# Two states of a selective scan in one tile, and where the last set's gating rows are kept

## The chip, the cores and the metric

The kernel runs on one core of a Trainium2 chip. A core has a matrix engine (PE, whose weight loads are listed apart as PEld), a vector engine (DVE), a scalar engine (ACT), a general engine (POOL) and a sequencer (SP) that here issues all DMAs. The engines run side by side and wait for each other by semaphores; each carries out its own instructions in the order in which they are listed. The metric is the time of one execution on the device in microseconds (us), the median of several runs.

## The reference, cut to what matters

An input of 8 batches of 512 tokens by 128 channels, x, goes through six residual blocks: an expert layer, an attention, the same expert layer, an attention with 16 gated experts (block "ea" in the kernel's names), a selective scan, and the 16 experts again ("eb"). Two of them are touched.

The scan, for each batch, with 256 channels d and 16 states n:

```
deltaA = exp(einsum('bld,dn->bldn', delta, A))
deltaB_u = (delta * u)[..., None] * Bm[:, :, None, :]
...
def step(h, t):
    dA_t, dBu_t, C_t = t
    h = dA_t * h + dBu_t
    return (h, jnp.einsum('bdn,bn->bd', h, C_t))
```

The end of the gated experts, where the attention's result is weighed by each expert's gate rw before the output product:

```
mixed = attn[:, :, None, :] * rw[..., None]
return jnp.einsum('bted,edc->btc', mixed, o_proj)
```

## The kernel before

Everything is one program for all 8 batches. The first three blocks run first (to about 360 us). After that two pipelines are interleaved: the scan of one batch after another (`scan_states`, two halves h of 128 channels each), and the expert blocks of other batches (`expert_qkv`, `expert_attend`), "ea" ahead of the scan of the same batch and "eb" behind it. The last set of all is "eb" of batch 7, named `ebg77`.

**The scan of one half** (`scan_states`, lines 936 to 1000) goes through the 16 states in 8 pairs m. For a pair, SP loads two tiles (line 967), `bn` and `cn`, each the rows of B or C of two states, repeated over 128 partitions (128x2x512, two buffers each). For each state: ACT makes `da` by an exponential (recorded at the helper's line 138), DVE multiplies the B row by `dup` into a PSUM bank `db` (line 977), DVE runs the recurrence over 512 tokens from `da` and `db` into an SBUF tile `hs` (line 980). Then POOL multiplies `hs` by its half of `cn` in place (line 983), and PE adds four transposes of it into the PSUM bank `ys` (line 986), which sums over the states. `hs` is one 128x512 tile for each state, six buffers. The generator gives up control (`yield`) after each ACT step, each DVE step, and each POOL multiplication.

**The end of an expert set** (`att_out`, lines 779 to 827): PE makes the attention output into PSUM (line 785), ACT copies it to `atT` (line 794). For each of 8 pairs m of experts, SP issues two DMAs that load the gate rows of the two experts from DRAM (`rwd`, written at line 624), each repeated over 64 partitions, into a 128x512 tile `pm` (line 803). `pm` has three buffers in the expert pool `ex`, so the loads of pair m=3 wait until the product of an earlier pair has been read. Then `mixed = pm * atT` (line 808, two buffers) on POOL; in the sets named in `QUICK`, `ebg77` among them, on DVE where m % 3 is not 0. PE multiplies `mixed` by the output weights (line 812, four token blocks for each m), DVE adds the result to x (line 822) and SP stores it (line 826).

**What sets the order.** The functions are generators, and `weave` first runs them in an order given by nominal times: each part has a start, an end and a number of steps (for `scan_states`, `3 + 4 * NS` in line 1449). `list_anew` then lists all instructions anew: it keeps a model of each engine's costs (`costs`: for POOL 2.125 ns an element and 185 ns), of buffers, and of a port that POOL and some DVE instructions share (`shares_port`), and lists each engine's instructions by the longest remaining way. One pass gives a plan, the second is built by it; so every instruction's place on its engine, and every buffer's place, comes out of this model. Buffers of the scan pool `sc` (tags `bn`, `cn`, `hs` and others) and the expert pool `ex` are tiles with fixed places, such as `bn_at0`.

Of the kernel before, what the change touches and what calls it, by code (L numbers as in the profile page):

```python
# [10 lines left out]
F32 = mybir.dt.float32  # L11
# [5 lines left out]
ALU = mybir.AluOpType  # L17
AX = mybir.AxisListType

P = 128  # L20
# [6 lines left out]

QKV_ACT = (1, 3, 5, 7)

QUICK, QKV_ACT_QUICK = ("eag00", "ebg77"), (0, 2, 4)  # L30

PART_BUFS, HS_BUFS, DA_BUFS, TAP_BUFS = 3, 3, 3, 2
# [28 lines left out]
def macaron_kernel(  # L61
# [19 lines left out]
    nc = tc.nc  # L81
    B, S, C = x_in.shape
# [5 lines left out]
    NH = 2  # L88
    NS = 16
# [37 lines left out]
    def behind(i, name, reason="table order"):  # L127
        i = getattr(i, "ins", i) if reason == "table order" else i
        order_only.append((i.name, name))
        tc.add_manual_dep(  # L130
            i,
            name,
            mybir.DependencyInfo(mybir.DependencyClass.NoSync, mybir.DependencyReason.DATA),
            reason=reason,
        )

    def act(*args, **kwargs):
        exp_ln.append(nc.scalar.activation(*args, **kwargs).ins.name)  # L138
# [321 lines left out]
    def scales_of(pool, psum, g, name, held):  # L460
        held[name, "scales"] = yield from ln_scales(pool, psum, g, name)
        yield
# [316 lines left out]
    def att_out(pool, psum, b, name, held, store):  # L779
        x, vv, den, rwd = xs[b], held[name, "vv"], held[name, "den"], held[name, "rwd"]  # L780
        sTs = [held[name, "sT", q] for q in range(J)]
        pat = psum("tr", [P, S], f"pat_{name}")
        for q in range(J):
            for k in range(q + 1):
                nc.tensor.matmul(
                    pat[:, q * P : (q + 1) * P],
                    lhsT=vv[:, k].rearrange("p i d -> p (i d)"),
                    rhs=sTs[q][:, k * P : (k + 1) * P],
                    start=k == 0,
                    stop=k == q,  # L790
                )
        yield
        atT = pool.tile([P, S], F32, tag="atT", name=f"atT_{name}", bufs=1)
        nc.scalar.copy(atT, pat)  # L794
        yield
        nc.vector.reciprocal(den, den)
        yield
        po = psum("tr", [P, J, C], f"po_{name}")
        for m in range(NE1 // 2):

            pm = pool.tile([P, S], F32, tag="pm", name=f"pm_{name}_{m}", bufs=3)
            for i in range(2):
                nc.sync.dma_start(
                    pm[i * HD1 : (i + 1) * HD1], rwd[2 * m + i : 2 * m + i + 1].to_broadcast([HD1, S])
                )
            mixed = pool.tile([P, S], F32, tag="mixed", name=f"mixed_{name}_{m}", bufs=2)
            engine = nc.vector if name in QUICK and m % 3 else nc.gpsimd
            engine.tensor_mul(mixed, pm, atT)  # L808
            yield
            for j in range(J):  # L810

                nc.tensor.matmul(  # L812
                    po[:, j, :],
                    lhsT=mixed[:, j * P : (j + 1) * P],
                    rhs=ow[:, m, :],
                    start=(m, j) == (0, 0),
                    stop=(m, j) == (NE1 // 2 - 1, J - 1),
                    skip_group_check=True,
                )
            yield  # L820
        for j in range(J):
            nc.vector.scalar_tensor_tensor(
                x[:, j, :], po[:, j, :], den[:, j : j + 1], x[:, j, :], ALU.mult, ALU.add
            )
        if store:
            nc.sync.dma_start(out[b].rearrange("(j p) c -> p j c", p=P), x)
        yield
# [108 lines left out]
    def scan_states(pool, psum, b, h, held):  # L936
        held[b, "delta", h]
        u, dl, du = (held[b, c][h] for c in ("u", "dl", "du"))
        z, bcd = held[b, "z"], held[b, "bcd"]

        ys = psum("ys", [P, J, P], f"ys_{b}_{h}")
        dup = psum("du", [P, S], f"dup_{b}_{h}")
        first = nc.scalar.copy(dup, du)
        if b + h:

            behind(first, held["late", NH * b + h - 1])
        yield

        scaled = nc.scalar.activation(u, u, AF.Copy, scale=cols[:, DSKIP + h : DSKIP + h + 1])
        behind(scaled, first.ins.name)  # L950
        for j in range(J):
            nc.tensor.matmul(
                ys[:, j, :],
                lhsT=u[:, j * P : (j + 1) * P],
                rhs=ident,
                is_transpose=True,
                start=j == 0,
                stop=False,
                skip_group_check=True,
            )  # L960
        yield
        for m in range(NS // 2):
            bn, cn = (
                pool.tile([P, 2, S], F32, tag=f"{c}n", name=f"{c}n_{b}_{h}_{m}", bufs=2) for c in "bc"
            )
            for t, r in ((bn, 2 * m), (cn, NS + 2 * m)):
                nc.sync.dma_start(
                    t, bcd[r : r + 2, :].rearrange("n s -> (n s)").unsqueeze(0).to_broadcast([P, 2 * S])
                )
            hs = [pool.tile([P, S], F32, tag="hs", name=f"hs_{b}_{h}_{m}_{i}", bufs=2 * HS_BUFS) for i in range(2)]  # L970
            for i in range(2):
                n = 2 * m + i
                db = psum("mm", [P, S], f"db_{b}_{n}_{h}")
                da = pool.tile([P, S], F32, tag="da", name=f"da_{b}_{n}_{h}", bufs=DA_BUFS)
                act(da, dl, AF.Exp, scale=a_neg[:, h * NS + n : h * NS + n + 1])
                yield
                product = nc.vector.tensor_mul(db, bn[:, i, :], dup)  # L977
                if n == NS - 3:
                    held["late", NH * b + h] = product.ins.name
                nc.vector.tensor_tensor_scan(hs[i], da, db, 0.0, ALU.mult, ALU.add)  # L980
                yield
            for i in range(2):
                nc.gpsimd.tensor_mul(hs[i], hs[i], cn[:, i, :])  # L983
                yield
                for j in range(J):
                    nc.tensor.matmul(  # L986
                        ys[:, j, :],
                        lhsT=hs[i][:, j * P : (j + 1) * P],
                        rhs=ident,
                        is_transpose=True,  # L990
                        start=False,
                        stop=(m, i, j) == (NS // 2 - 1, 1, J - 1),
                        skip_group_check=True,
                    )
            if m == NS // 2 - 1:
                yield
                zh = z[:, :, h * P : (h + 1) * P]
                nc.vector.tensor_mul(zh, ys, zh)
                held[b, "yz", h] = True
            yield  # L1000
# [438 lines left out]
    def scan_parts(pool, psum, t, b, held):  # L1439
        pieces = [(0.05, 0.0, 1, scan_normed(pool, psum, b, held)), (0.1, 0.0, 1, scan_begin(pool, b, held))]  # L1440
        for h in range(NH):
            pieces.append((0.15 + 0.1 * h, 0.0, 1, scan_conv(pool, psum, b, h, held)))
        for i in range(2):
            pieces.append((0.35 + 0.1 * i, 0.45 + 0.1 * i, 3, scan_gate(psum, b, i, held)))
        pieces += [(0.55, 0.0, 1, scan_rows(pool, psum, b, held)), (0.6, 0.0, 1, scan_rank(pool, psum, b, held))]
        pieces.append((0.7, 0.0, 1, scan_silu(b, held)))
        for h in range(NH):
            pieces.append((0.8 + 0.1 * h, 0.0, 1, scan_delta(pool, psum, b, h, held)))
        states = [(0.5 * h, 0.5 + 0.5 * h, 3 + 4 * NS, scan_states(pool, psum, b, h, held)) for h in range(NH)]
        states += [(1.0 + 0.02 * h, 0.0, 1, scan_turn(pool, psum, b, h, held)) for h in range(NH)]  # L1450
        states += [(1.04, 1.12, J + 2, scan_finish(psum, b, held))]
        return (
            [(t - 0.24 * SLOT_T, t - 0.24 * SLOT_T, 1, scales_of(pool, psum, (b,), f"ss{b}", held))]
            + spread(t - 0.22 * SLOT_T, t, pieces)
            + spread(t, t + SLOT_T, states)
        )
# [12 lines left out]
    def psum(tag, shape, name):  # L1469
        return psp.tile(shape, F32, tag="bank", name=name, bufs=8)  # L1470
# [12 lines left out]
    sc = Buffers(behind_pools(first, "sc", "left"), dict(xn=1, xps=1))  # L1483
# [110 lines left out]
    parts, held, t = [], Held(), 0.0  # L1594
# [79 lines left out]
```

## Time and profile before

| what | value |
|---|---|
| median of 3 runs (lowest to highest) | 1281.96 us (1279.81 to 1287.47) |
| profiled execution: its own time, its span | 1279.87 us, 1278.1 us |
| busy in the span: PE, DVE, POOL, ACT | 1101.5, 1065.3, 935.9, 851.5 us |
| POOL multiplications at line 983 | 256 of 1280 ns |
| DVE scans at line 980 | 256 of 1210 ns |
| busy in 400 to 1200 us (800 us): PE, DVE, POOL | 690.3, 714.0, 673.4 us |
| granted PE clock, mean | 0.929 |

A row of the page's groups has the line, engine and operation, what is written and read, the shape, the count, then the busy time and the mean of one, then the idle time of the engine just before such instructions and what ended most of it. A row of the timeline has start, length, engine, line, operation and count, and in square brackets the idle time before it and who ended it. The chain is the sequence of waits and work that ended last, followed back from the end.

### The profile page before, as it was taken

Reading aid. Unit: us, or ns where it says so; the run is one execution under the profiler, and the core shown is the slowest. Engines: PE = TensorE matmul, PEld = TensorE weight load, DVE = VectorE, ACT = ScalarE, POOL = GpSimd, SP = SyncE. Lnnn points to the kernel's source line nnn. Section 1 sums busy time; section 2 is a strip of 40 time slices with the busy share of each in tenths; the row PEclk is TensorE's granted clock in tenths of the full one; section 3 lists DMA queues with packets and bytes.
Section 4 is the critical chain, followed back from the end, with each engine's and each line's share of the span. In section 5 each row is a group of like instructions: output and inputs, shape, how many; then the busy total and the mean of one; then the engine's idle time right before and its main releaser. Section 6 shows DMA issues by size and latency. Waiting matters only on the chain.

```text
span 1278.1 us, 20254 instructions
## 1 busy us (share of the span) xinstructions
PE 1101.5 (86%) x6242; PEld 907.4 (71%) x6242; DVE 1065.3 (83%) x2613; ACT 851.5 (67%) x1953; POOL 935.9 (73%) x784
## 2 busy tenths in 40 slices
PE   6988899999897877788989989899897769988875
PEld 5767778678675765666868878687785657777665
DVE  7997666987789999998989979989985998899462
ACT  4788873675587778565886687686577458865321
POOL 5685532764489898883999889789989857888641
PEclk9999998999899998896999989799998969989797
DMA  5000000000175776754556646545765872476211
GB/s 150 25 9 1 1 1 1 1 28 22 47 218 197 215 248 213 235 183 134 190 177 210 216 147 215 168 149 205 232 202 169 259 238 96 132 236 209 79 65 50
DMA packets 69215, 178.05 MB, mean 139 GB/s; under 512 B 9585, under 2 KB 18162, under 8 KB 69106
## 3 DMA queue, kind: packets, MB, share of 16 engines
q1 hardware_dynamic: 69106, 176.75, 43.0%
q8 instruction: 49, 0.80, 0.3%
q14 instruction: 60, 0.49, 0.1%
HBM read 173.57 MB, written 3.15 MB: 138 GB/s over the span
## 4 chain that ended last, share of the span: by engine, by line
PE 30%; DVE 27%; ACT 16%; POOL 10%; issue 9%; DMA 6%; SPq 1%; POOLq 0%; DVEq 0%; ACTq 0%
PE bank_at L251 15%; DVE hs_at L980 9%; DVE bank_at L977 5%; DVE qkv_at L661 3%; POOL hs_at L983 3%; PE bank_at L986 3%; PE bank_at L812 2%; ACT part_at L675 2%; DVE x L436 2%; DMA bn_at<-bcd 2%; POOL sums_at L690 2%; ACT my_at L440 2%; PE bank_at L358 2%; DMA pm_at<-rwd_ebg 2%; ACT da_at L138 1%
## 5 line engine op out<-in xcount | busy, mean ns | idle before, releaser
L983 POOL TENSOR_TENSOR hs_at<-hs_at,cn_at 128x512 f32<-128x512 f32 x256 | 323.8, 1280 | 73.7 <-DVE hs_at L980 23.0
L980 DVE TENSOR_TENSOR_SCAN hs_at<-da_at,bank_at 128x512 f32<-128x512 f32 x256 | 306.2, 1210 | 5.1 <-PE bank_at L986 1.2
L138 ACT ACTIVATE da_at<-dl_at,a_neg 128x512 f32<-128x512 f32 x256 | 184.8, 725 | 104.7 <-DVE hs_at L980 100.4
L675 ACT ACTIVATE part_at<-bank_at,rw_at 128x192 f32<-128x192 f32 x496 | 177.8, 424 | 83.4 <-PE bank_at L251 70.1
L986 PE MATMUL bank_at<-ident,hs_at 128*128 128x128 f32 x1024 | 181.7, 298 | 33.9 <-POOL hs_at L983 32.4
L808 POOL TENSOR_TENSOR mixed_at<-pm_at,atT_at 128x512 f32<-128x512 f32 x118 | 150.9, 1287 | 54.6 <-ACT atT_at L794 27.0
L661 DVE SCALAR_TENSOR_TENSOR qkv_at<-bank_at,rw_at,qkv_at 128x192 f32<-128x192 f32 x464 | 174.2, 408 | 19.0 <-PE bank_at L251 12.9
L977 DVE TENSOR_TENSOR bank_at<-bn_at,bank_at 128x512 f32<-128x512 f32 x256 | 172.3, 686 | 20.5 <-DMA bn_at<-bcd 6.0
L690 POOL TENSOR_TENSOR sums_at<-sums_at,part_at 128x768 f32<-128x768 f32 x92 | 170.1, 1848 | 20.5 <-ACT part_at L675 19.0
L812 PE MATMUL bank_at<-ow,mixed_at 128*128 128x128 f32 x1024 | 163.6, 298 | 21.7 <-POOL mixed_at L808 20.6
L986 PEld LDWEIGHTS bank_at<-ident,hs_at 128*128 128x128 f32 x1024 | 133.0, 153 | 55.8 <-POOL hs_at L983 50.3
L812 PEld LDWEIGHTS bank_at<-ow,mixed_at 128*128 128x128 f32 x1024 | 146.8, 207 | 33.4 <-POOL mixed_at L808 30.6
L251 PE MATMUL bank_at<-pw_hi,xha_at 128*128 128x384 f32 x256 | 98.5, 402 | 20.2 <-DVE hs_at L980 8.6
L251 PE MATMUL bank_at<-pw_hi,xhb_at 128*128 128x384 f32 x256 | 97.1, 400 | 11.5 <-DVE rw_at L609 2.9
L446 POOL TENSOR_TENSOR my_at<-my_at,my_at 128x512 f32<-128x512 f32 x48 | 62.4, 1302 | 39.4 <-ACT my_at L440 35.2
L440 ACT ACTIVATE my_at<-bank_at,moe_w_at 128x128 f32<-128x128 f32 x256 | 71.9, 401 | 27.1 <-PE bank_at L251 23.8
L251 PE MATMUL bank_at<-pw_lo,xha_at 128*128 128x384 f32 x256 | 85.0, 348 | 0.0
L251 PE MATMUL bank_at<-pw_hi,xla_at 128*128 128x384 f32 x256 | 83.9, 352 | 0.0
L251 PE MATMUL bank_at<-pw_lo,xhb_at 128*128 128x384 f32 x256 | 83.9, 344 | 0.0
L436 DVE SCALAR_TENSOR_TENSOR x<-bank_at,moe_w_at,x 128x128 f32<-128x128 f32 x256 | 78.0, 342 | 6.9 <-PE bank_at L251 6.0
L251 PE MATMUL bank_at<-pw_hi,xlb_at 128*128 128x384 f32 x256 | 79.7, 344 | 0.0
L863 POOL TENSOR_TENSOR u_at<-u_at,tap_at 128x511 f32<-128x511 f32 (+1 forms) x48 | 61.4, 1279 | 24.9 <-issue 16.0
(269 smaller groups left out, 2614.4 us busy)
## 6 DMA issues: line engine op xcount, KB each, us to landing
bn_at<-bcd SPq DMA_DIRECT2D x128, 512.0 KB, 4.5
cn_at<-bcd SPq DMA_DIRECT2D x128, 512.0 KB, 4.6
pm_at<-rwd_eag SPq DMA_DIRECT2D x128, 128.0 KB, 3.6
pm_at<-rwd_ebg SPq DMA_DIRECT2D x128, 128.0 KB, 3.4
x<-x_in_dram SPq DMA_DIRECT2D x8, 256.0 KB, 4.4
out_dram<-x SPq DMA_DIRECT2D x8, 256.0 KB, 2.9
pw<-proj_w_dram SPq DMA_DIRECT2D x6, 256.0 KB, 2.8
ew<-expert_w_dram SPq DMA_DIRECT2D x1, 512.0 KB, 6.4
```

The lines of the kernel that those rows point to most:

```text
L138: exp_ln.append(nc.scalar.activation(*args, **kwargs).ins.name)
L251: nc.tensor.matmul(out, lhsT=lhs[a], rhs=rhs[b], start=first and k == 0, stop=final and k == 2)
L436: nc.vector.scalar_tensor_tensor(x[:, j, :], pe[:, i, :], w[:, j, k : k + 1], x[:, j, :], ALU.mult, ALU.add)
L661: nc.vector.scalar_tensor_tensor(qkv, v, rw[:, i : i + 1], qkv, ALU.mult, ALU.add)
L675: nc.scalar.activation(held[name, "parts", h][i][:, j, :], pp[:, i, :], AF.Copy, scale=rw[:, i : i + 1])
L690: nc.gpsimd.tensor_add(sums, sums, t)
L808: engine.tensor_mul(mixed, pm, atT)
L812: nc.tensor.matmul(po[:, j, :], lhsT=mixed[:, j * P : (j + 1) * P], rhs=ow[:, m, :], start=(m, j) == (0, 0), stop=(m, j) == (NE1 // 2 - 1, ...
L977: product = nc.vector.tensor_mul(db, bn[:, i, :], dup)
L980: nc.vector.tensor_tensor_scan(hs[i], da, db, 0.0, ALU.mult, ALU.add)
L983: nc.gpsimd.tensor_mul(hs[i], hs[i], cn[:, i, :])
L986: nc.tensor.matmul(ys[:, j, :], lhsT=hs[i][:, j * P : (j + 1) * P], rhs=ident, is_transpose=True, start=False, stop=(m, i, j) == (NS // 2 ...
```

## The change

In `scan_states` the two states of a pair get one tile `hs` of 128x2x512 (three buffers, so the same bytes); each scan writes its half; POOL multiplies the whole tile by the whole of `cn` in one instruction, after both scans; then come the transposes of both states, eight for each bank. The nominal number of steps becomes `3 + 3 * NS`. In `att_out`, for `ebg77` alone, the rows `pm` are put two pairs to a tile of the shape and tags of `bn` and `cn` in the scan pool: four tiles hold all eight pairs.

```
+LAST = "ebg77"
...
-            pm = pool.tile([P, S], F32, tag="pm", name=f"pm_{name}_{m}", bufs=3)
+            if name == LAST:
+
+                if not m % 2:
+                    c = "bc"[m // 2 % 2]
+                    pms = sc.tile([P, 2, S], F32, tag=f"{c}n", name=f"pm_{name}_{m}", bufs=2)
+                pm = pms[:, m % 2, :]
+            else:
+                pm = pool.tile([P, S], F32, tag="pm", name=f"pm_{name}_{m}", bufs=3)
...
-            hs = [pool.tile([P, S], F32, tag="hs", name=f"hs_{b}_{h}_{m}_{i}", bufs=2 * HS_BUFS) for i in range(2)]
+            hs = pool.tile([P, 2, S], F32, tag="hs", name=f"hs_{b}_{h}_{m}", bufs=HS_BUFS)
...
-                nc.vector.tensor_tensor_scan(hs[i], da, db, 0.0, ALU.mult, ALU.add)
+                nc.vector.tensor_tensor_scan(hs[:, i, :], da, db, 0.0, ALU.mult, ALU.add)
                 yield
+            nc.gpsimd.tensor_mul(hs, hs, cn)
+            yield
             for i in range(2):
-                nc.gpsimd.tensor_mul(hs[i], hs[i], cn[:, i, :])
-                yield
                 for j in range(J):
                     nc.tensor.matmul(
                         ys[:, j, :],
-                        lhsT=hs[i][:, j * P : (j + 1) * P],
+                        lhsT=hs[:, i, j * P : (j + 1) * P],
...
-        states = [(0.5 * h, 0.5 + 0.5 * h, 3 + 4 * NS, scan_states(pool, psum, b, h, held)) for h in range(NH)]
+        states = [(0.5 * h, 0.5 + 0.5 * h, 3 + 3 * NS, scan_states(pool, psum, b, h, held)) for h in range(NH)]
```

## The prediction

> **What bounds the kernel now.** I read the page from the top: busy shares, the chain that ended last, the costliest groups. Then the busy times by stretch, who waits for whom between 400 and 1200 us (the scan), and the timeline of the last 53 us.
>
> ```profile
> PE 1101.5 (86%) x6242; PEld 907.4 (71%) x6242; DVE 1065.3 (83%) x2613; ACT 851.5 (67%) x1953; POOL 935.9 (73%) x784
> PE 30%; DVE 27%; ACT 16%; POOL 10%; issue 9%; DMA 6%; SPq 1%; POOLq 0%; DVEq 0%; ACTq 0%
> L983 POOL TENSOR_TENSOR hs_at<-hs_at,cn_at 128x512 f32<-128x512 f32 x256 | 323.8, 1280 | 73.7 <-DVE hs_at L980 23.0
> L980 DVE TENSOR_TENSOR_SCAN hs_at<-da_at,bank_at 128x512 f32<-128x512 f32 x256 | 306.2, 1210 | 5.1 <-PE bank_at L986 1.2
> L690 POOL TENSOR_TENSOR sums_at<-sums_at,part_at 128x768 f32<-128x768 f32 x92 | 170.1, 1848 | 20.5 <-ACT part_at L675 19.0
> L986 PE MATMUL bank_at<-ident,hs_at 128*128 128x128 f32 x1024 | 181.7, 298 | 33.9 <-POOL hs_at L983 32.4
> ```
>
> No engine is the bound alone. PE, DVE and POOL are all near full in the scan and the chain changes between them. POOL holds 10% of it, and the page gives 3% of the span (38 us) to line 983. DVE almost never waits for an `hs` buffer (1.2 us in all).
>
> ```profile
> core 0: us, PE busy (x) PEld busy (x) DVE busy (x) ACT busy (x) POOL busy (x), PEclk, DMA share, GB/s
> 700.00:800.00 100.00, 93.58 (x592) 79.48 (x591) 87.38 (x199) 73.23 (x167) 90.44 (x68) 0.97 0.60 191
> 800.00:900.00 100.00, 91.44 (x541) 76.67 (x541) 93.00 (x194) 72.36 (x160) 83.88 (x64) 0.93 0.56 180
> 900.00:1000.00 100.00, 87.52 (x529) 72.16 (x529) 80.18 (x133) 69.42 (x145) 90.42 (x69) 0.93 0.61 195
> ```
>
> From one 100 us stretch to the next the busiest engine changes: DVE at 800 to 900, POOL at 900 to 1000.
>
> The second edit lies in the tail, where little else runs:
>
> ```profile
> 1230.67 38.26 SPq L803 DMA_DIRECT2D pm_at<-rwd_ebg  x16
> 1258.98 1.77 POOL L808 TENSOR_TENSOR mixed_at<-pm_at,atT_at 128x512 f32<-128x512 f32 x1 [18.67 <-ACT atT_at L794]
> 1262.05 0.69 DVE L808 TENSOR_TENSOR mixed_at<-pm_at,atT_at 128x512 f32<-128x512 f32 x1 [2.42 <-PE bank_at L812]
> 1265.27 1.26 POOL L808 TENSOR_TENSOR mixed_at<-pm_at,atT_at 128x512 f32<-128x512 f32 x1 [4.53 <-DMA pm_at<-rwd_ebg]
> 1270.29 1.26 POOL L808 TENSOR_TENSOR mixed_at<-pm_at,atT_at 128x512 f32<-128x512 f32 x1 [3.75 <-DMA pm_at<-rwd_ebg]
> 1271.61 2.05 PE L812 MATMUL bank_at<-ow,mixed_at 128*128 128x128 f32 x16 [0.45 <-POOL mixed_at L808]
> ```
>
> The sixteen loads are spread over 38 us because they wait for the three `pm` buffers, and POOL's products of m=3 and m=6 wait for rows (4.53 and 3.75 us). The chain runs through both waits.
>
> **First edit: one POOL instruction for two states.** What does it save? Instructions that follow each other directly overlap a little, so I use the distance between starts:
>
> ```profile
> 700.67 1.83 POOL L687 TENSOR_TENSOR sums_at<-part_at,part_at 128x768 f32<-128x768 f32 x1
> 702.47 1.27 POOL L808 TENSOR_TENSOR mixed_at<-pm_at,atT_at 128x512 f32<-128x512 f32 x1
> 703.71 4.97 POOL L983 TENSOR_TENSOR hs_at<-hs_at,cn_at 128x512 f32<-128x512 f32 x4
> ```
>
> A 128x768 takes 702.47 - 700.67 = 1.80 us, a 128x512 703.71 - 702.47 = 1.24 us, and four in 4.97 us agree, (4.97 - 1.28)/3 = 1.23. So 256 elements more cost 0.56 us, and 128x1024 should take 1.24 + 2 x 0.56 = 2.36 us against 2.48 us for two: 0.12 us saved for a pair, and 128 pairs make 15 us of POOL's 936. By the durations (1848 - 1280 = 568 ns for 256) it is 2560 - 2416 = 144 ns a pair, 18 us.
>
> Not all of this reaches the end. The least: only where line 983 is on the chain, 38 us / 2.48 = 15 pairs x 0.12 = 1.8 us. The most: POOL binds everywhere, 15 us. I take the share of the scan in which POOL is busier than DVE by these rows, the two stretches 700 to 800 and 900 to 1000 out of eight: 15 x 2/8 = 3.8 us, which is nearest to the chain's value.
>
> What does it cost? A product now waits for both scans. The first state's transposes come later by one DVE product and one scan, 0.69 + 1.21 = 1.90 us, and by the longer instruction, 2.36 - 1.24 = 1.12 us, together 3.0 us; the second state's, where POOL is free, by 1.12 us. On PE, all that is listed behind these transposes waits with them; the profile has this wait already (32.4 us in 37 waits between 400 and 1200 us). Behind the longer POOL instruction, other POOL work (the sums at line 690, `mixed`, the taps) can be held up to 1.12 us longer. SP's next load of `cn` starts when the product has been read, 1.12 us later, but the row itself is needed 1.90 us later, so POOL's 18.2 us of waits for `cn` should not grow. `hs` buffers: a pair lives from its first scan to its last transpose, two (scan + product) 3.8, POOL 2.36, eight transposes of 0.27 or 2.2: about 8.4 us; three pairs last 3 x 6.25 = 18.8 us at the mean pace of 32 states in 100 us. So DVE's wait for `hs` stays small; without that slack each late pair would cost DVE, the busiest engine of the stage, its 3.0 us directly.
>
> In the longest pieces of the chain I find a scan followed directly by its line 983 five times (412, 522, 605, 887, 907 us). Bounds of the cost: 0 if PE has other work each time; 5 x 1.12 = 5.6 us if none. I take the half, 2.8 us. Far off lies the case that PE starves; it is a rival below.
>
> The changed generator and the changed step count also make the listing place all instructions anew. The trace can't show what another order gives; I bound it by two neighbouring stretches, DVE busy 93.0 against 80.2 in 100 us: one such stretch won or lost is 13 us either way. I put it at zero, the middle, and keep half, 6.5 us, as the width of the forecast.
>
> One rule speaks against longer POOL instructions. In the tail POOL's product took 1.77 us instead of 1.28 while DVE ran one with two SBUF inputs (1258.93). The Trainium skill, "SBUF — State Buffer", section "SBUF: two separate sides", says that such a DVE instruction and a POOL one take turns at a shared port pair, held for the whole instruction. By it a 2.36 us product would block DVE for up to 2.36 us. But during the scan DVE's products, scans and line 661 each read one operand from PSUM, so by the rule the sum gets nothing.
>
> **Second edit: all rows of the last set at once.** The rows in DRAM are written by line 624 at 1227.42; the first load follows at 1230.67. The last scan's readers of `bn` and `cn` end at 1191, so the four places are free. Sixteen issues of 0.45 to 0.60 us end near 1239, and with 3.4 us to land all rows are there by 1243, long before `atT` (1258.93); an issue is hidden under 15 us of qkv matmuls, and without that cover it would cost its 8.6 us. Only the last store is behind them on SP.
>
> What is late next is the two `mixed` buffers. PE takes 1.0 us for one m (2.05 us for two). Following on from the rows of before: m=2 on DVE at 1262.05 as now; m=3 on POOL when PE has done m=1, 1263.0 to 1264.3, PE to 1265.3; m=4 on DVE at 1264.0, PE to 1266.4; m=5 at 1265.4, PE to 1267.4; m=6 on POOL when m=4 is done, 1266.45 to 1267.7, PE to 1268.8; m=7 to 1269.8. PE now ends at 1271.61 + 2.05 = 1273.66: gain 3.9 us. Bounds: 0 if the order of before stays bound elsewhere, 4.9 if PE ran eight times 1.0 us without a gap from 1260.80.
>
> **Sum** against the profiled execution's 1279.87 us (2.1 below the median 1281.96): -3.8 + 2.8 - 3.9 = -4.9, so 1275.
>
> **The rivals.** *PE starves (slower).* Place: PE's in-order queue at line 986. If half of the 37 waits, 18, grow by 3.0 us without other work, that is 55 us, and with PE's 30% of the chain 16.5 us: 1279.87 + 16.5 - 3.9 = 1292. It decides from the point where these waits outweigh the gains: (3.8 + 3.9) / (0.3 x 3.0) = 9 such waits. For it: PE and PEld wait for line 983 longer than for nearly anything else. Against: PE has idle time in the scan, 800 - 690 = 110 us, and work of other batches.
>
> *POOL binds everywhere.* All 15 us and the tail: 1279.87 - 15 - 3.9 = 1261. For it: POOL at 90% in three stretches. Against: DVE is busier over the whole scan, 714 against 673 us in 800.
>
> *The second edit does nothing.* The `mixed` buffers or a later place in the listing hold the tail as it is: 1275 + 3.9 = 1279. Against: `DMA` ends the two waits, and the loads fit by 16 us.
>
> **How the numbers follow.** Forecast 1275, own range 1268 to 1282 (6.5 either way): 0.45. PE starves, 1292, spread 1286 to 1300: 0.25. POOL binds, 1261, spread 1255 to 1268: 0.20. Tail unchanged, 1279: 0.10. About 1% is what a measurement of this kernel can tell from no change; against 1281.96 that is below 1269.1 or above 1294.8. Faster: all of the POOL rival and 0.10 of the forecast's lower edge, 0.30. Slower: 0.17 of PE starving. Same: 0.53. The range leaves out 0.08 of the POOL rival and 0.12 of PE starving: 1258 to 1296.
>
> **What would show it.** Line 983: 128 rows of 128x1024 near 2.4 us (2.5 or more refutes the saving). POOL busy near 918 to 921. PE's waits for line 983 in 400 to 1200 us: near 32 us in the forecast, over 60 if PE starves. SP's sixteen loads at line 803 in under 10 us, no wait of POOL for `pm` in the tail, and PE's products at line 812 from first to last in 9.0 us instead of 12.9. DVE's wait at line 980 for line 986 over 10 us would mean that three pair buffers are too few. The prediction is wrong if the scan's stretch (360 to 1190 us) moves by more than 10 us: then the order of the listing, not the instruction's price, decides.

## The result, and the profile after

| | before | changed |
|---|---|---|
| median | 1281.26 us (1279.81 to 1287.47, 4 runs) | 1310.56 us (1308.25 to 1315.68, 4 runs) |
| ratio to before, 95% interval | | 1.0232 (1.0203 to 1.0261) |
| profiled execution: time, span | 1279.87, 1278.1 us | 1309.9, 1308.1 us |

The change is 29 us slower; the forecast was 1275 and its range ended at 1296. In the changed kernel the scan is at line 988, POOL's product at 990, the transposes at 994, `mixed` at 816, its matmuls at 820, the loads of `pm` at 811. From its page, busy times, chain by engine, and groups:

```profile
PE 1103.1 (84%) x6242; PEld 913.5 (70%) x6242; DVE 1071.4 (82%) x2613; ACT 852.7 (65%) x1953; POOL 917.4 (70%) x656
PE 31%; DVE 28%; ACT 18%; issue 10%; POOL 7%; DMA 5%; SPq 1%; POOLq 0%; DVEq 0%; ACTq 0%
L990 POOL TENSOR_TENSOR hs_at<-hs_at,cn_at 128x1024 f32<-128x1024 f32 x128 | 303.7, 2374 | 94.6 <-DVE hs_at L988 54.1
L988 DVE TENSOR_TENSOR_SCAN hs_at<-da_at,bank_at 128x512 f32<-128x512 f32 x256 | 306.0, 1210 | 2.7 <-PE bank_at L252 0.6
L994 PE MATMUL bank_at<-ident,hs_at 128*128 128x128 f32 x1024 | 176.1, 304 | 54.5 <-POOL hs_at L990 54.3
```

The work of PE, DVE and ACT is the same within 1%, and POOL's is 18.5 us less: 128 products of 2374 ns for 256 of 1280. No engine's work accounts for the 30 us of span: they are time in which the engines stand. Over the same 800 us of the scan each does less than before (of POOL's 36 us some are the merger's own saving).

```profile
core 0: us, PE busy (x) PEld busy (x) DVE busy (x) ACT busy (x) POOL busy (x), PEclk, DMA share, GB/s
400.00:1200.00 800.00, 668.29 (x3939) 557.19 (x3939) 699.28 (x1391) 549.31 (x1182) 637.31 (x373) 0.91 0.59 189
```

(Before: PE 690.3, DVE 714.0, POOL 673.4; the granted clock, 0.91, is the same in both. Over the whole span it was 0.929 and 0.920.)

The waits around the product, two rows before and two after, with the total in us, the number of waits and the longest, from 400 to 1200 us:

```profile
PE bank_at L986 <- POOL hs_at L983: 32.4, 37, 3.1
POOL hs_at L983 <- DVE hs_at L980: 22.7, 16, 3.0
```

```profile
PE bank_at L994 <- POOL hs_at L990: 48.5, 38, 3.0
POOL hs_at L990 <- DVE hs_at L988: 54.1, 18, 18.1
```

PE's waits for the products grew by 16 us. POOL's waits for the scans grew by 31 us in almost as many waits; one of them is 18.1 us long.

Where in time? The end of a half scan, the product at line 998 before and 1006 after, is a good mark. Start in us, from the timelines:

| half scan | 1st | 6th | 9th | 11th | 16th | end of span |
|---|---|---|---|---|---|---|
| before | 413.9 | 644.2 | 827.3 | 942.4 | 1192.9 | 1278.1 |
| changed | 422.0 | 672.5 | 831.5 | 965.8 | 1225.4 | 1308.1 |
| difference | 8.1 | 28.3 | 4.2 | 23.4 | 32.5 | 30.0 |

The loss is not spread evenly, as a dearer step in each pair would be: it jumps, falls back and jumps again. And it begins before the scan. The rows of line 980 before and of 988 after, with the first and last start:

```profile
L980 DVE TENSOR_TENSOR_SCAN hs_at<-da_at,bank_at x256: 1190/1210/1222, 365.3 to 1186.9; 128x512 f32<-128x512 f32 x128
```

```profile
L988 DVE TENSOR_TENSOR_SCAN hs_at<-da_at,bank_at x256: 1192/1210/1223, 372.3 to 1217.8; 128x512 f32<-128x512 f32 x128
```

The first scan starts 7.0 us later, after 365 us of a program in which the change touches no instruction. Part of this can be the difference between two executions. In the four profiles whose kernels keep the order of before (before itself and three runs of the next section) it starts at 365.3 to 367.3 us, in the four with the changed kernel's order (itself and three such runs) at 371.3 to 372.6: some 4 us or more come from the order. The longest gap between the two scans of a pair, on the timelines of DVE and POOL after, lies in one of the jumps:

```profile
834.58 1.21 DVE L988 TENSOR_TENSOR_SCAN hs_at<-da_at,bank_at 128x512 f32<-128x512 f32 x1
...
850.99 0.69 DVE L985 TENSOR_TENSOR bank_at<-bn_at,bank_at 128x512 f32<-128x512 f32 x1
851.58 0.41 DVE L662 SCALAR_TENSOR_TENSOR qkv_at<-bank_at,rw_at,qkv_at 128x192 f32<-128x192 f32 x1
851.91 0.41 DVE L660 TENSOR_SCALAR qkv_at<-bank_at,rw_at 128x192 f32<-128x192 f32 x1
852.24 1.21 DVE L988 TENSOR_TENSOR_SCAN hs_at<-da_at,bank_at 128x512 f32<-128x512 f32 x1
```

```profile
853.58 2.38 POOL L990 TENSOR_TENSOR hs_at<-hs_at,cn_at 128x1024 f32<-128x1024 f32 x1 [18.14 <-DVE hs_at L988]
```

The two scans of one pair stand 17.7 us apart; before, the longest such gap was 9.7 us (828.93 to 838.65). The second one's input product (line 985) carries no bracket: DVE comes to it straight from the instruction ahead of it, in the place it was listed at. Meanwhile POOL stood for 18.14 us. This is one place, as an example; how the 30 us are made up place by place is not shown.

### The profile page after: what moved, and what is told of

Same layout as the page of the kernel before. It is cut to its first block, busy times and chain, and to the rows that moved or that the text cites. A ratio compares the mean times of both kernels' runs of the same rounds, so it can differ in the third digit from the quotient of the medians.

```text
span 1308.1 us, 20001 instructions
## 1 busy us (share of the span) xinstructions
PE 1103.1 (84%) x6242; PEld 913.5 (70%) x6242; DVE 1071.4 (82%) x2613; ACT 852.7 (65%) x1953; POOL 917.4 (70%) x656
## 3 DMA queue, kind: packets, MB, share of 16 engines
HBM read 173.57 MB, written 3.15 MB: 135 GB/s over the span
## 4 chain that ended last, share of the span: by engine, by line
PE 31%; DVE 28%; ACT 18%; issue 10%; POOL 7%; DMA 5%; SPq 1%; POOLq 0%; DVEq 0%; ACTq 0%
PE bank_at L252 15%; DVE hs_at L988 8%; DVE bank_at L985 5%; DVE qkv_at L662 3%; DMA bn_at<-bcd 3%; PE bank_at L994 3%; POOL hs_at L990 3%; ACT part_at L676 3%; DVE x L437 2%; PE bank_at L820 2%; PE bank_at L786 2%; ACT my_at L441 1%; PE bank_at L773 1%; POOL sums_at L691 1%; ACT xn_at L336 1%
## 5 line engine op out<-in xcount | busy, mean ns | idle before, releaser
L990 POOL TENSOR_TENSOR hs_at<-hs_at,cn_at 128x1024 f32<-128x1024 f32 x128 | 303.7, 2374 | 94.6 <-DVE hs_at L988 54.1
L988 DVE TENSOR_TENSOR_SCAN hs_at<-da_at,bank_at 128x512 f32<-128x512 f32 x256 | 306.0, 1210 | 2.7 <-PE bank_at L252 0.6
L994 PE MATMUL bank_at<-ident,hs_at 128*128 128x128 f32 x1024 | 176.1, 304 | 54.5 <-POOL hs_at L990 54.3
L816 POOL TENSOR_TENSOR mixed_at<-pm_at,atT_at 128x512 f32<-128x512 f32 x115 | 147.2, 1289 | 39.2 <-issue 12.8
L820 PE MATMUL bank_at<-ow,mixed_at 128*128 128x128 f32 x1024 | 157.8, 292 | 16.7 <-POOL mixed_at L816 14.3
L820 PEld LDWEIGHTS bank_at<-ow,mixed_at 128*128 128x128 f32 x1024 | 140.9, 202 | 28.7 <-POOL mixed_at L816 25.2
L252 PE MATMUL bank_at<-pw_hi,xha_at 128*128 128x384 f32 x256 | 102.6, 415 | 25.1 <-DVE qkv_at L662 7.5
L252 PE MATMUL bank_at<-pw_hi,xlb_at 128*128 128x384 f32 x256 | 83.0, 349 | 0.0
L252 PEld LDWEIGHTS bank_at<-pw_hi,xha_at 128*128 128x128 f32 x256 | 50.3, 199 | 45.6 <-DVE qkv_at L662 13.0
```

The source lines that it names most:

```text
L252: nc.tensor.matmul(out, lhsT=lhs[a], rhs=rhs[b], start=first and k == 0, stop=final and k == 2)
L820: nc.tensor.matmul(po[:, j, :], lhsT=mixed[:, j * P : (j + 1) * P], rhs=ow[:, m, :], start=(m, j) == (0, 0), stop=(m, j) == (NE1 // 2 - 1, ...
L988: nc.vector.tensor_tensor_scan(hs[:, i, :], da, db, 0.0, ALU.mult, ALU.add)
L990: nc.gpsimd.tensor_mul(hs, hs, cn)
L994: nc.tensor.matmul(ys[:, j, :], lhsT=hs[:, i, j * P : (j + 1) * P], rhs=ident, is_transpose=True, start=False, stop=(m, i, j) == (NS // 2 ...
```

## The experiments

Two theories were set against each other. **Order**: the change makes the listing place all instructions anew, and this order is worse than that of before. **Pair wait**: the product that waits for both scans holds PE and POOL. In these kernels the scan is at line 998, the product at 1003, 1007 or 1011, the transposes at 1014, the tail's products at 822, their matmuls at 826 and loads at 817. Medians of one kernel differ by some us from chip to chip, so the ratio to before, measured on the same chip, is what is compared.

### One edit at a time

The second edit alone (the lines that take effect):

```
-            hs = pool.tile([P, 2, S], F32, tag="hs", name=f"hs_{b}_{h}_{m}", bufs=HS_BUFS)
+            hs = [pool.tile([P, S], F32, tag="hs", name=f"hs_{b}_{h}_{m}_{i}", bufs=2 * HS_BUFS) for i in range(2)]
...
-            nc.gpsimd.tensor_mul(hs, hs, cn)
...
+                nc.gpsimd.tensor_mul(hs[i], hs[i], cn[:, i, :])
```

> The second edit alone: the scan as before, the last set's rows at once; every engine's order is that of before, except for the sixteen loads. Prediction's step: the tail shortens by 3.9 us, so about 1277. Rival (the tail gains nothing): 1281.

Measured: 1280.35 us, ratio 0.9967 (0.9944 to 0.9989), so -4.2 us. In the traces, PE, ACT and DVE carry out the same operations in the same sequence as before. Its tail, on POOL's and PE's timelines:

```profile
1261.19 1.76 POOL L822 TENSOR_TENSOR mixed_at<-bn_at,atT_at 128x512 f32<-128x512 f32 x1 [18.56 <-ACT atT_at L801]
1265.15 1.27 POOL L822 TENSOR_TENSOR mixed_at<-cn_at,atT_at 128x512 f32<-128x512 f32 x1 [2.19 <-PE bank_at L826]
1268.60 1.27 POOL L822 TENSOR_TENSOR mixed_at<-cn_at,atT_at 128x512 f32<-128x512 f32 x1 [2.19 <-PE bank_at L826]
```

```profile
1263.01 3.16 PE L826 MATMUL bank_at<-ow,mixed_at 128*128 128x128 f32 x24 [2.52 <-POOL mixed_at L822]
1266.47 3.16 PE L826 MATMUL bank_at<-ow,mixed_at 128*128 128x128 f32 x24 [0.30 <-POOL mixed_at L822]
1269.93 2.05 PE L826 MATMUL bank_at<-ow,mixed_at 128*128 128x128 f32 x16 [0.30 <-POOL mixed_at L822]
```

Both waits for `pm` are gone. What is late next is PE's reading of the `mixed` buffers (2.19 us), and the products run from 1263.01 to 1271.98, 8.97 us against 12.86. This edit does what it says, but not all of these 3.9 us are the waits. Before, PE's second 24 were dear too:

```profile
1266.59 4.57 PE L812 MATMUL bank_at<-ow,mixed_at 128*128 128x128 f32 x24 [2.63 <-POOL mixed_at L808]
```

They took 4.57 us at a granted clock of 0.64 (1266.5 to 1271.2 us), here 3.16. PE's standing time between the products fell by 2.5 us (2.63 + 0.45 before, 0.30 + 0.30 here); the other 1.4 us are this difference.

The first edit alone. In these kernels `ORDER_OF` names the version that is listed and `RUN_AS` the one whose instructions are run; the first value of each stands for the merged product, the second for the rows at once:

```
+ORDER_OF, RUN_AS = (True, False), (True, False)
...
-            if name == LAST:
+            if name == LAST and rows_at_once:
```

> The first edit alone, in the order that it gets in the changed kernel; the last set's rows in three buffers as before. If the two edits are independent and the tail is worth 3.9 us: about 1314. If the tail gains nothing: 1310.

Measured: 1315.32 us, ratio 1.0243 (1.0206 to 1.0280). The loss, 31 us, is the first edit's. The two effects add up to 27 us and the changed kernel lost 30; the intervals are some 3 to 5 us wide each way, so nothing speaks against the edits being independent.

### The order kept, the instruction changed

Four kernels take an order from one version and the instructions from another. `list_anew` is run for the one, and each instruction's turn is noted by its part, its engine and its number there; for the other, instructions are listed by these turns wherever what they depend on allows it:

```
+        if follow is not None:
...
+            while open_:
+                v, k = heapq.heappop(open_)
...
+                    behind(work[k], last[e], "listed")
```

The changed kernel's order, each product split into the two of before (`ORDER_OF, RUN_AS = (True, True), (False, True)`):

```
-                nc.gpsimd.tensor_mul(hs[2], hs[2], cn)
+                for i in range(2):
+                    nc.gpsimd.tensor_mul(hs[i], hs[i], cn[:, i, :])
```

> The changed kernel with every engine's order kept, instruction by instruction, but each product of 128x1024 given back as two of 128x512 in the same place, the first of which waits for the first scan alone. Theory 'order' (the loss comes from the new listing): it stays near the changed kernel, 1305 to 1318. Rival 'pair wait' (the loss comes from the product that waits for both scans): it falls back by most of the 29 us, to 1281 to 1290.

Measured: 1310.31 us, ratio 1.0203 (1.0161 to 1.0246). In its trace PE, DVE and ACT carry out the same operations in the same sequence as in the changed kernel. Its waits, of PE from 400 to 1200 us and of POOL from 400 to 1240 us:

```profile
PE bank_at L1014 <- POOL hs_at L1007: 27.1, 32, 2.5
```

```profile
POOL hs_at L1007 <- DVE hs_at L998: 44.4, 22, 16.1
```

PE now waits less for the products than before the change (27.1 against 32.4 us), and still nothing of the loss that can be told from noise comes back (1.0203 against 1.0232, intervals of 0.004 each way). POOL's longest wait for a scan, 16.1 us, stays. The pair's wait is not what costs 29 us in this order.

The same with two halves of the tokens, which both wait for both scans:

```
+                for half in (slice(0, S // 2), slice(S // 2, S)):
+                    nc.gpsimd.tensor_mul(hs[2][:, :, half], hs[2][:, :, half], cn[:, :, half])
```

> The changed kernel with every engine's order kept, but each product of 128x1024 as two of 128x2x256, each with one half of the tokens of both states: both wait for both scans, and only the saving of one instruction for a pair is gone. If POOL's 15 us are worth 3.8 us as predicted: about 1314. If they are worth nothing at the end: 1310, as the changed kernel. If they bound the kernel: 1325.

Measured: 1308.16 us, ratio 1.0177 (1.0153 to 1.0202). POOL's products are back at 256 of 1278 ns and its busy time in the span at 934.2 us, yet the kernel is not slower than the changed one. So POOL's time does not bound the kernel. It is even some 7 us faster by the ratios, and one thing besides POOL's time differs: PE can begin with the first half's transposes before the second half is multiplied. Where POOL's two halves run from 501.74 to 504.24 us, PE's transposes start at 503.69, and PE's waits for the products are 39.4 us instead of 48.5. So a gain of a few us from the saving, such as the 3.8 of the prediction, is neither shown nor excluded.

Now the other way round, the order of before with merged products; the first state's transposes move only where they stood ahead of the product. The `hs` buffers are then three tiles for pairs instead of six for states:

```
+ORDER_OF, RUN_AS = (False, False), (True, False)
```

> The kernel before with every engine's order kept as it was, but each pair's two products replaced by one of 128x1024 in the place of the second; the first state's transposes move behind it only where they stood ahead of it. Theory 'order': near before, 1275 to 1290. Rival 'pair wait': 1305 or more.

Measured: 1362.15 us, ratio 1.0610 (1.0563 to 1.0657), 78 us slower. This is what the rival expected (1305 or more), and far outside what the theory of the order did. PE's waits from 400 to 1200 us:

```profile
PE bank_at L1014 <- POOL hs_at L1003: 87.1, 60, 4.0
```

The pair's wait is real: in an order made for early products PE stands at transposes that can't start, 87.1 us instead of 32.4. So I moved these transposes:

```
+                if key is not None and key[0] in scan_parts_at and key[1] == ENG.PE and key[2] >= J:
+                    m, rest = divmod(key[2] - J, 2 * J)
+                    if rest < J:
+                        asked_by[k] = follow[key[0], key[1], J + 2 * J * m + J] - 0.5 + 0.05 * rest
```

> As the run with the order of before and merged products (1362), but on PE the first state's four transposes of each pair are moved back to stand just ahead of the second state's. Theory 'PE's queue is held' (the 80 us of that run are PE standing at transposes that were listed for an earlier product): most of it comes back, to 1285 to 1305. Rival (the longer instruction or the late product itself delays the other engines): it stays above 1330.

Measured: 1317.35 us, ratio 1.0235 (1.0192 to 1.0279). By the ratios 48 of the 78 us come back. In its profiled execution, the fastest of its four (1308.82 us), PE's waits at the transposes are at 38.9 us, and DVE's wait for an `hs` buffer, 1.2 us before, is 7.8. It missed both expectations. What the other 30 us are, in an order that was made for other products, was not taken further.

### The same work in another order

If the order is worth tens of us, then another order alone must show it. `DVE_WAY` weighs DVE's instructions in the remaining way by which the listing ranks them; it changes no instruction. At five other weights, picked by hand, both versions were run: "rows" is the second edit alone (the scan of before), "both" is the changed kernel.

```
-DVE_WAY = 1.3
+DVE_WAY = 1.35
```

> The scan of before with the second edit, as in the run of the rows alone (1280); the only difference is the listing's weight for DVE's remaining way, 1.35 instead of 1.30, so the work is the same instruction by instruction and only the engines' orders change. Theory 'order' (another order alone costs as much as what was measured): 5 to 25 us slower than 1280. Rival 'pair wait' (the order is worth little): 1277 to 1285.

> The changed kernel, with the weight 1.35 and nothing else different. Theory 'order': it leaves 1310 by more than 10 us, to 1285 to 1300, and lies within 12 us of the run with the scan of before at the same weight. Rival 'pair wait': 1305 to 1315, and 25 to 30 us above that run.

> The scan of before with the second edit, the weight 1.20. Theory 'order': 1285 to 1305. Rival 'pair wait': 1277 to 1285.

> The changed kernel, the weight 1.20. Theory 'order': 1285 to 1305, within 12 us of the run with the scan of before at that weight. Rival 'pair wait': 25 to 30 us above it.

> The scan of before with the second edit, the listing's weight 1.15; the work is the same. Theory 'order only' (the first edit costs nothing in a fresh listing): 1285 to 1305, and level with its partner within 6 us in the mean over the pairs. Rival 'order and pairing' (a pair costs about 8 us in any listing, the rest of the 29 is the order): its partner is 8 us slower in the mean over all pairs of weights.

> The changed kernel, the weight 1.15. 'Order only': in the mean over the pairs level with the scan of before at the same weight. 'Order and pairing': 8 us slower in the mean.

> The scan of before with the second edit, the weight 1.25. Expectations as at 1.15.

> The changed kernel, the weight 1.25. Expectations as at 1.15.

> The scan of before with the second edit, the listing's weight 1.40; the work is the same. 'Order only': 1285 to 1305, level with its partner in the mean over the pairs. 'Order and pairing': its partner is 8 us slower in the mean over the pairs.

> The changed kernel, the weight 1.40. 'Order only': level with its partner in the mean over the six pairs. 'Order and pairing': 8 us slower in the mean.

Measured, median and ratio to before with its interval:

| weight | rows | both | difference of ratios |
|---|---|---|---|
| 1.15 | 1302.91, 1.0164 (1.0136 to 1.0191) | 1314.65, 1.0259 (1.0225 to 1.0294) | +0.0095 |
| 1.20 | 1301.26, 1.0139 (1.0101 to 1.0177) | 1295.84, 1.0094 (1.0060 to 1.0129) | -0.0045 |
| 1.25 | 1283.12, 1.0015 (0.9991 to 1.0040) | 1287.43, 1.0047 (1.0019 to 1.0074) | +0.0032 |
| 1.30 | 1280.35, 0.9967 (0.9944 to 0.9989) | 1310.56, 1.0232 (1.0203 to 1.0261) | +0.0265 |
| 1.35 | 1298.10, 1.0114 (1.0085 to 1.0143) | 1297.98, 1.0116 (1.0080 to 1.0152) | +0.0002 |
| 1.40 | 1293.86, 1.0078 (1.0049 to 1.0107) | 1309.34, 1.0189 (1.0134 to 1.0243) | +0.0111 |

Identical work costs from 0.9967 to 1.0164, 25 us, by its order alone (with the buffers' places that come with it). The weight of before, 1.30, is the best of the six for the scan of before, by 6 us from the next and 17 us from the mean of the other five (1.0102). For the changed scan it is the second worst. At 1.35 the versions are level, at 1.20 the changed one is 6 us faster by the medians, with intervals that overlap. Of the expectations, "rows" at 1.25 was missed by 2 us on the good side (1285 to 1305); "both" at 1.20 and 1.35 lies where the theory of the order put it.

PE's waits for the products say the same: at the five other weights they are 29.9 to 41.1 us for the merged products and 31.7 to 37.8 us for the separate ones. A listing can place merged products without making PE wait more. Some of an order's cost may go with the clock: "rows" had a median granted clock of 0.926 at 1.30, and 0.909 at 1.15 and 1.35. This was not separated.

Is there a cost of the pairing in any order? The six differences have a mean of 0.0077, or 9.8 us, with a standard error of 0.0044. Without 1.30, the weight at which the question arose, the five have a mean of 0.0039, 5 us, with a standard error of 0.0029. The expectations had set 0 us against 8 us for the mean of the six, and 9.8 lies nearer to 8; but with so few pairs the 95% interval reaches from -5 to 24 us for the six and from -5 to 15 us for the five. Both ideas fit, so a cost of the pairing stays open; it is not the whole 29.

Two more orders, with the weight of PE's costs in the listing lowered as well:

```
-SLOW = 1.15
+SLOW = 1.1
...
-DVE_WAY = 1.3
+DVE_WAY = 1.24
```

> The scan of before with the second edit, listed with other weights (1.24 for DVE's way, 1.10 for PE's cost); the work is the same. Theory 'order': another order may also be faster than that of before; 1268 to 1290. Rival 'pair wait': 1277 to 1285, as with any order.

> The changed kernel listed with other weights (1.27 and 1.10), the work is that of the change. Theory 'order': 1275 to 1295, well below its 1310. Rival 'pair wait': 1305 or more.

Measured: rows at 1.24 and 1.10, 1283.64 us, ratio 0.9973 (0.9950 to 0.9995); both at 1.27 and 1.10, 1298.81 us, 1.0098 (1.0069 to 1.0126). The changed scan again leaves its 1310 by a mere change of order, though less far than was expected (1275 to 1295). The scan of before at 1.24 and 1.10 is as fast as in the order of before (0.9973 and 0.9967), so that order is not alone in being good. No order tried makes the changed scan faster than before. Only these two versions of the second edit alone have intervals below before.

## Why the prediction was wrong

**The step that failed** is the one about the listing: "one such stretch won or lost is 13 us either way. I put it at zero, the middle, and keep half, 6.5 us, as the width of the forecast." The reach was too small and the centre was wrong. Orders of the same work differ by 25 us, and zero is not the middle when the order of before is one of the best: the other five weights cost the same work 17 us in the mean (15 us over six with the order at 1.24 and 1.10), and the changed kernel's own order lies some 12 us above the mean of its other five (1.0232 against 1.0141). With 5 us of pairing, if it is that, and -4 of the tail, this makes up 30 us. These parts are differences of the same table and must add up, so the sum is a way of dividing the loss, not a proof of each part. That this one order is among the bad ones is chance as far as the runs show: a slightly different weight gives 1287 or 1298 us. The new step count and the dependency on both scans come with the change together; which of them turned the order was not separated. The range ended at 1296 because 16.5 us of a starving PE were its upper end, and the order was not added to it.

**Point by point.** The price of the merged product was right: 2374 ns measured, 2.36 and 2.42 us by the two workings, and POOL's busy time 917.4 us where 918 to 921 were expected. What it would bring, 3.8 us, is seen in no run; the experiments can't tell it from nothing. POOL's share of the chain was the sign for little; that POOL is busier than DVE in two stretches does not show that it bounds them.

The tail's waits were right: they are gone, 9.0 us from first to last matmul were worked out and 8.97 measured in the second edit alone, the gain 3.9 against 4.2 us. That the number fits so well is in part luck. The working took 1.0 us of PE for every m; the 24 of m=3 to 5 had taken 4.57 us before and took 3.16 in that run, so 1.4 of the 3.9 us came from a term that the working did not have. In the changed kernel it fell out the other way: its tail took 10.4 us, since PE's first 24 took 4.41 us at a granted clock of 0.67. The sixteen loads took 10.0 us from the first issue to the end of the last, in both kernels, just over the "under 10" that was named, and 0.63 us each where 0.45 to 0.60 were assumed; nothing waited for them.

Buffers: DVE's wait for `hs` stays under 1 us in the changed kernel, as expected.

**The rivals.** "PE starves" forecast the sign, by a wrong mechanism for this kernel. PE's waits for the products grew from 32.4 to 48.5 us, below the 60 that was named as its mark, and the split version has 27.1 us of them and is as slow. Where it is right is the order of before: there merging costs 78 us, and 48 of them come back when PE's transposes are moved. A new listing avoids that. "POOL binds" is refuted by the half-token products, which cost POOL its time again and the kernel nothing (1308 us where 1325 was expected of it). The rule on the shared port was rightly given nothing: DVE's scans took 1210 ns before and after.

The last sentence of the prediction held: the scan's stretch moved by 24 us (1217.8 - 372.3 against 1186.9 - 365.3), "then the order of the listing, not the instruction's price, decides".

## What to carry to other kernels

Where a planner lists the whole program anew, a change of one cost or one dependency is a change of every engine's order; the cost of that need not lie around zero, since the order in hand can be one of the best, as it was here. Measure it: nudge a weight that changes no instruction, and compare old and new at several weights, or keep the order and change the instruction alone. POOL, 84% busy in the scan and with 10% of the chain, gave nothing back that could be measured for 18 us less work.

## What the runs showed of the hardware that was not expected

The same matmuls at the same place can run at two speeds, and a stand of some 2.5 us does not decide which. In the changed kernel's tail 24 records of line 820 took 4.41 us at a mean granted clock of 0.67 from 1293 to 1298 us, and the next 24 took 3.15 us at 1.00:

```profile
1293.25 4.41 PE L820 MATMUL bank_at<-ow,mixed_at 128*128 128x128 f32 x24 [2.52 <-POOL mixed_at L816]
```

In the second edit alone the same 24, after the same stand of 2.52 us, took 3.16 us at 1.00; so did the first 24 before, and there it was the next 24, after 2.63 us, that took 4.57 us at 0.64. So the tail's gain, 3.9 us by the traces in the second edit alone, was 2.4 us (12.86 - 10.42) in the changed kernel. What sets the clock here is not shown.
